# Expert outputs collected in two ways: the first 40 experts through zeroed rows that are summed during the last twelve pairs, the other 24 through three sums in DRAM

## The chip, the core and the metric

The kernel runs on one core of a Trainium2 chip. TensorE (PE) multiplies and transposes, VectorE (DVE) and ScalarE (ACT) work on tiles, GpSimd (POOL) issues the indirect DMAs, and SyncE (SP) issues most of the others. SBUF is the on-chip memory with 128 partitions, PSUM receives what PE computes, DRAM lies outside. The metric is the time of one execution in microseconds, lower is better; each version is timed in several executions and the median counts.

## What is computed

One transformer block on x of shape (2, 512, 256): 1024 tokens of 256 channels. A mixing layer comes first, then a mixture of 64 small experts, of which each token uses 6, beside a shared expert that all tokens use. Cut to what matters here:

```python
router_logits = x @ gate_w.T
probs = softmax(router_logits)                      # 1024 x 64
topk_w, topk_idx = top_k(probs, 6)
topk_w = topk_w / sum(topk_w)
combine = sum(one_hot(topk_idx, 64) * topk_w[..., None], axis=1)
h = silu(einsum('th,eih->tei', x, experts_w1))      # 64 experts, 176 wide
y = einsum('tei,ehi->teh', h, experts_w2)
routed_out = einsum('teh,te->th', y, combine)
ffn = routed_out + shared_out
out = x + layernorm(ffn)
```

Only the six chosen experts of a token are computed. So every token has six rows of 256 numbers, made by six experts at different times, and these have to be added before the last layernorm.

## The kernel before

**Mixing and routing (0 to 136 us of the span).** Eight tiles of 128 tokens pass through the mixing layer, get their router logits and their top six. Each tile then sends its token rows to the experts: `xs_d` in DRAM has 1024 row places for each expert, and six indirect DMAs (scatters, line 576) per tile write each token's row to the next free place of each of its experts, 48 scatters in all. A row (`ROW` = 384 floats, 1536 bytes) holds the 256 normalized channels, 64 combine weights and 64 integers. The integer of expert e says which row of `y_d` the output for this token and expert belongs to: row 6 x token + k. A scan over the chosen experts (`tok[:, t, DEST:]`) makes these numbers. Before that, the first 128 places of each expert are filled with `blank`, a row with zero weights and row numbers that are out of bounds, so that empty places write nothing.

On SP's queue stand, in this order: the inputs, four fills of `xs_d` with `blank` (line 173), the shared expert's weights, the weights of the first 11 pairs of experts, a copy of the token rows to `tok_d` in two halves (lines 706 and 719) with the weights of pairs 11 and 12 between them, and then the loop's loads.

**Expert pairs (136 to 266 us).** 32 pairs of experts, two at a time, in a software pipeline that is written out by hand. In step n of the loop at the end of `block_kernel`:

- SP issues the load of pair n + 4 from `xs_d` (`load`, tile `xg`, five buffers);
- `turn_h` transposes the hidden values of pair n - 2 on PE and copies them to SBUF on DVE (lines 921 to 925);
- `turn` transposes the token rows of pair n on PE (line 887); DVE copies the weight and row-number columns (`cols`, line 891) and the transposed rows (`xT`, line 893);
- `up` multiplies pair n - 1 by its first weights (line 906), ACT applies SiLU (lines 911 and 912);
- `down` multiplies pair n - 2 by its second weights (lines 933 and 937), ACT scales by the combine weights (line 940) into `y`, which has six buffers, and `collect` issues one indirect DMA per expert that writes its up to 128 rows to `y_d` (line 864). These are the puts, two for each pair;
- SP issues further weights, until all are loaded.

An expert with more than 128 tokens has its surplus computed by `further`, one extra block of 128 rows spread over steps 3 to 8 of the loop. After the loop stands a hardware loop (`tc.For_i`, line 1007) for still more surplus, which turns zero times with this data. All engines and all DMAs meet at it.

**Tail (272 us to the end).** For each of the eight token tiles, 768 KB of `y_d` (six rows for each token) are loaded into `yk`, half by a DMA of SP and half by one of ACT (line 1021); these wait for every put. `total_up` adds the upper three rows to the lower three on DVE (line 1032), and PE adds `y_sh` (the shared expert, line 1029) and the three sums (line 1034) by multiplying with the identity and accumulating in PSUM. `measure` takes mean and variance, `put_out` normalizes, adds x and writes the tile out (line 1057); for the last two tiles this is done on DVE, for the others on ACT and POOL.

Of the kernel before, what the change touches and what calls it, by code (L numbers as in the profile page):

```python
# [10 lines left out]
F32 = mybir.dt.float32  # L11
BF16 = mybir.dt.bfloat16
I32 = mybir.dt.int32
# [5 lines left out]
P = 128  # L19
# [16 lines left out]
FLOAT = 1  # L36
G = 2
NG = E // G
DEST = C + E
ROW = DEST + E  # L40
WROW = 2 * I + C
HALF = P // 2
SEL = 131072.0
# [9 lines left out]
def block_kernel(ctx: ExitStack, tc, x, w_act, w_rec, w_val, gate, wa, wb, wb_one, sh_gu, sh_dn, out):  # L53
# [110 lines left out]

    blank = const.tile([P, ROW], F32, name="blank")
    nc.gpsimd.memset(blank[:, :DEST], 0.0)
    nc.gpsimd.iota(blank[:, DEST:].bitcast(I32), pattern=[[0, E]], base=int(FAR), channel_multiplier=0)


    xs_d = dram.tile([E * CAP, ROW], F32, name="xs_d")  # L170
# [10 lines left out]

    
    first_i = const.tile([P, NTT], I32, name="first_i")
    for i in range(NTT):
        nc.gpsimd.iota(
# [157 lines left out]
    def spent(n):  # L345
        return 0.16 + n / 960
# [93 lines left out]

    hsh = carve(len(SH_CHUNKS), NT)
    tok = carve(NTT, ROW)
    sel = data.tile([P, NTT, E], BF16, name="sel")
    lg = data.tile([P, NTT, E + 10], F32, name="lg")
    nc.gpsimd.memset(lg[:, :, E : E + 2], NEG)
    none_sel = const.tile([P, E], BF16, name="none_sel")
# [26 lines left out]
    def token_tile(t, pv):  # L473
# [79 lines left out]
        for j in range(t):  # L553
# [5 lines left out]
        yield spent(E / 2)  # L559

        nc.vector.tensor_tensor_scan(
            tok[:, t, DEST:].bitcast(I32), sel[:, t, :], none_sel, first_f[:, t : t + 1], ALU.add, ALU.add
        )
        yield spent(2 * E)

        nc.vector.reciprocal(tsum, tsum)
        nc.scalar.activation(comb, comb, AF.Copy, scale=tsum)
# [188 lines left out]
    def further(now, f):  # L756
# [64 lines left out]
        nc.vector.tensor_mul(two, xg[:, C:DEST], one)  # L821
        wt = stat.tile([P, 1], F32, tag="wt", name="wt")
        nc.vector.tensor_reduce(wt, two, AX.X, ALU.add)
        nc.vector.tensor_mul(two, xg[:, DEST:].bitcast(I32), one)
        to = stat.tile([P, 1], F32, tag="to", name="to")
        nc.vector.tensor_reduce(to, two, AX.X, ALU.add)
        to_i = stat.tile([P, 1], I32, tag="to_i", name="to_i")
        nc.vector.tensor_copy(to_i, to)
        yield
        px = ps.tile([P, KC, P], F32, tag="ps", name="px")  # L830
        for k in range(KC):
# [19 lines left out]
        nc.tensor.matmul(py, hT[:IB, 1, :], wb_f, start=False, stop=True)  # L851
        y = hpool.tile([P, C], F32, tag="y_f", name="y_f", bufs=1)
        nc.scalar.activation(y, py, AF.Copy, scale=wt)
        collect(y, to_i)
        yield

    def after_scatters(ins):
# [5 lines left out]
    def collect(y, rows):  # L863
# [10 lines left out]
        tc.add_to_no_dep_group("puts", ins)  # L874
        puts.append(ins)

    def load(g):
        xg = hpool.tile([P, G, ROW], F32, tag="xg", name="xg", bufs=5)
        after_scatters(nc.sync.dma_start(xg, xs_v[:P, g * G : (g + 1) * G, :]).ins)
        return xg  # L880

    def turn(xg, g):

        px = ps.tile([P, G, KC, P], F32, tag="pr", name="px", bufs=1)
        for q in range(G):
            for k in range(KC):
                nc.tensor.transpose(px[:, q, k, :], xg[:, q, ts(k, P)], ident)  # L887
        cols = hpool.tile([P, 2, G], F32, tag="cols", name="cols", bufs=12)
        flat = xg.rearrange("p q r -> p (q r)")
        for u, o in enumerate((C + g * G, DEST + g * G)):  # L890
            nc.vector.tensor_copy(cols[:, u, :].bitcast(I32), flat[:, o : o + ROW + 2 : ROW + 1].bitcast(I32))
        xT = hpool.tile([P, G, KC, P], F32, tag="xT", name="xT")
        nc.vector.tensor_copy(xT, px)  # L893
        return xT, cols
# [30 lines left out]
        nc.vector.tensor_copy(hT[: HALF + IB, G, :], pt[: HALF + IB, G, :])  # L925
        return hT

    def down(hT, w2as, w2b, wts, rows):

        pys = []  # L930
        for q in range(G):
            py = ps.tile([P, C], F32, tag="ps", name="py")
            nc.tensor.matmul(py, hT[:, q, :], w2as[q], start=True, stop=False)  # L933
            pys.append(py)
        for q in range(G):
            lo = q * HALF
            nc.tensor.matmul(pys[q], hT[lo : lo + IB, G, :], w2b[lo : lo + IB, :], start=False, stop=True)  # L937
        y = hpool.tile([P, G, C], F32, tag="y", name="y", bufs=6)
        for q in range(G):
            nc.scalar.activation(y[:, q, :], pys[q], AF.Copy, scale=wts[q])  # L940
            collect(y[:, q, :], rows[q])


    floats = []
# [16 lines left out]
    warm = ps.tile([P, C], F32, tag="ps", name="warm")  # L961
    for i in range(5):
        nc.tensor.matmul(warm, ident, x_sb[:, 0, :], start=(i == 0), stop=(i == 4))

    AHEAD = 4
    xgs, xTs, hs, hTs, cols = {}, {}, {}, {}, {}
# [3 lines left out]
    for n in range(NG + 2):  # L970
        if n + AHEAD < NG:
            xgs[n + AHEAD] = load(n + AHEAD)
        if FIRST + 2 + n < FIRST + SECOND:
            load_weights(FIRST + 2 + n)
        if 0 <= n - 2 < NG:
            hTs[n - 2] = turn_h(hs.pop(n - 2))
        if n < NG:
            xTs[n], cols[n] = turn(xgs.pop(n), n)
        float_step(n)
        if 0 <= n - 1 < NG:  # L980
            wa_sb, wb_sb = weights[n - 1]
            hs[n - 1] = up(xTs.pop(n - 1), [wa_sb[:, q, : 2 * I] for q in range(G)])
        if 0 <= n - 2 < NG:
            m = n - 2
            wa_sb, wb_sb = weights[m]
            col = cols.pop(m)
            down(
                hTs.pop(m),
                [wa_sb[:, q, 2 * I :] for q in range(G)],
                wb_sb,  # L990
                [col[:, 0, q : q + 1] for q in range(G)],
                [col[:, 1, q : q + 1] for q in range(G)],
            )
# [13 lines left out]
    with tc.For_i(0, left, 1):  # L1007
# [4 lines left out]

    hstack.close()
    tpool = ctx.enter_context(tc.tile_pool(name="tpool", bufs=3))
    y_v = y_d.rearrange("(i p k) c -> p i k c", k=TOPK, p=P)
    half = TOPK // 2
    yks, pos, mvs, rstds = {}, {}, {}, {}
    for i in range(NTT):
        yks[i] = tpool.tile([P, TOPK, C], F32, tag="yk", name="yk", bufs=NTT)
        for eng, o in ((nc.sync, 0), (nc.scalar, half)):  # L1020
            ins = eng.dma_start(yks[i][:, o : o + half, :], y_v[:, i, o : o + half]).ins
            for w in puts:
                tc.add_manual_dep(ins, w.name, SYNC, reason="reads what every block wrote")

    def total_up(i):

        yk = yks.pop(i)
        po = pos[i] = ps.tile([P, C], F32, tag="ps", name="po")
        nc.tensor.matmul(po, ident, y_sh[:, i, :], start=True, stop=False)
        pieces = [(0, half)] if i < NTT - 2 else [(k, k + 1) for k in range(half)]  # L1030
        for o, u in pieces:
            nc.vector.tensor_add(yk[:, o:u, :], yk[:, o:u, :], yk[:, half + o : half + u, :])  # L1032
        for k in range(half):
            nc.tensor.matmul(po, ident, yk[:, k, :], start=False, stop=(k == half - 1))  # L1034

    def measure(i):
        mv = mvs[i] = stat.tile([P, 2], F32, tag="mv_o", name="mv_o")
# [69 lines left out]
```

## Time and profile before

| | us |
|---|---|
| median of 4 runs | 301.35 |
| lowest and highest run | 298.26 and 301.86 |
| the profiled execution | 301.84 |
| its span, first to last instruction | 300.1 |
| mean granted TensorE clock | 0.886 |

The profile's times are us from the start of the span. Busy shares of the span are PE 80%, DVE 50%, ACT 40% and POOL 42%, but they mix three stages with different limits: the mixing stage, where chains between engines alternate and the DMA queues are full for the first 75 us, the pair loop, and the tail. The stages are read one by one with the view that gives the busy time of each engine in chosen stretches, and with the timeline. In the view of waits, the longest wait of the pair loop is this one:

```profile
DVE hT L924 <- PE pht L922: 67.6, 30, 3.5
```

It says that DVE waited 67.6 us in total, in 30 of the 32 steps, for PE's transposes of the hidden values.

### The profile page before, as it was taken

Reading aid. Unit: us, or ns where it says so; the run is one execution under the profiler, and the core shown is the slowest. Engines: PE = TensorE matmul, PEld = TensorE weight load, DVE = VectorE, ACT = ScalarE, POOL = GpSimd, SP = SyncE. Lnnn points to the kernel's source line nnn. Section 1 sums busy time; section 2 is a strip of 40 time slices with the busy share of each in tenths; the row PEclk is TensorE's granted clock in tenths of the full one; section 3 lists DMA queues with packets and bytes.
Section 4 is the critical chain, followed back from the end, with each engine's and each line's share of the span. In section 5 each row is a group of like instructions: output and inputs, shape, how many; then the busy total and the mean of one; then the engine's idle time right before and its main releaser. Section 6 shows DMA issues by size and latency. Waiting matters only on the chain. (4 is left out here: it accounts for less than half of the span.)

```text
span 300.1 us, 4388 instructions
## 1 busy us (share of the span) xinstructions
PE 239.3 (80%) x1258; PEld 190.0 (63%) x1258; DVE 149.6 (50%) x628; ACT 120.0 (40%) x341; POOL 125.3 (42%) x159
## 2 busy tenths in 40 slices
PE   1989824954877929995898999999999999921992
PEld 0778613843665717874676778888888877710881
DVE  3569899756768503760345323344433333201594
ACT  3494665256127336502134444433333333320241
POOL 6000006723741761773064465555555555550041
PEclk9999975887597775995999999999999999995697
DMA  7999999999662440637999999999855531115982
GB/s 227 379 401 400 389 331 347 394 387 327 263 221 99 157 155 35 233 131 261 352 344 352 358 362 364 363 357 346 264 159 154 155 116 54 54 54 203 407 307 79
DMA packets 44025, 77.58 MB, mean 259 GB/s; under 512 B 4885, under 2 KB 29578, under 8 KB 44000
## 3 DMA queue, kind: packets, MB, share of 16 engines
q1 hardware_dynamic: 36480, 58.04, 56.6%
q0 software_dynamic: 6368, 16.11, 14.6%
q10 hardware_dynamic: 1152, 3.15, 2.9%
q8 instruction: 10, 0.16, 0.2%
q14 instruction: 15, 0.12, 0.1%
HBM read 46.53 MB, written 33.16 MB: 266 GB/s over the span
## 5 line engine op out<-in xcount | busy, mean ns | idle before, releaser
L864 POOL DMA_INDIRECT y_d<-y,cols x64 | 63.1, 987 | 66.2 <-ACT y L940 54.1
L576 POOL DMA_INDIRECT xs_d<-arena,slot_i x48 | 48.0, 999 | 81.3 <-ACT lg L526 40.9
L924 DVE COPY hT<-pht 128x256 f32<-128x256 f32 x32 | 13.6, 424 | 69.2 <-PE pht L922 67.6
L940 ACT ACTIVATE y<-py,cols 128x256 f32<-128x256 f32 x64 | 26.8, 470 | 29.2 <-PE py L937 27.4
L911 ACT ACTIVATE h<-ph 128x256 f32<-128x256 f32 x32 | 12.3, 383 | 47.7 <-PE ph L906 40.1
L906 PE MATMUL ph<-w_sb,xT 128*128 128x176 f32 x176 | 30.0, 313 | 0.0
L599 PE MATMUL pgu<-x2T,sh_gu_sb 128*128 128x256 f32 (+1 forms) x96 | 27.9, 453 | 0.0
L906 PEld LDWEIGHTS ph<-w_sb,xT 128*128 128x128 f32 x176 | 26.4, 190 | 0.3 <-issue 0.3
L893 DVE COPY xT<-px 128x512 f32<-128x512 f32 x32 | 21.9, 685 | 4.3 <-PE px L887 4.3
L599 PEld LDWEIGHTS pgu<-x2T,sh_gu_sb 128*128 128x128 f32 (+1 forms) x96 | 20.4, 217 | 4.9
L395 DVE TENSOR_TENSOR m<-z 128x32 f32<-128x32 f32 (+7 forms) x92 | 22.0, 281 | 2.4 <-remote 1.8
L933 PE MATMUL py<-w_sb,hT 128*128 128x256 f32 x88 | 22.7, 380 | 0.0
L458 PE MATMUL pv<-w_val_sb,z 128*128 128x256 f32 x32 | 12.7, 565 | 11.7 <-DVE z L398 7.8
L887 PE MATMUL px<-ident,xg 128*128 128x128 f32 x128 | 19.3, 273 | 0.8 <-DVE xT L893 0.8
L264 PE MATMUL pz<-xnT,arena 128*128 128x256 f32 x64 | 17.4, 434 | 1.7 <-ACT xnT L253 1.0
L458 PEld LDWEIGHTS pv<-w_val_sb,z 128*128 128x128 f32 x32 | 8.6, 281 | 14.1 <-issue 9.8
L1034 PE MATMUL po<-yk,ident 128*128 128x256 f32 x48 | 14.1, 436 | 3.7 <-DVE yk L1032 3.7
L264 PEld LDWEIGHTS pz<-xnT,arena 128*128 128x128 f32 x64 | 13.8, 220 | 4.9 <-ACT xnT L253 1.4
L933 PEld LDWEIGHTS py<-w_sb,hT 128*128 128x128 f32 x88 | 15.8, 190 | 1.2
L887 PEld LDWEIGHTS px<-ident,xg 128*128 128x128 f32 x128 | 15.0, 141 | 1.2 <-DVE xT L893 1.0
L921 PE MATMUL pht<-ident,h 128*128 128x128 f32 x64 | 14.0, 301 | 2.0 <-ACT h L911 2.0
L283 PE MATMUL pr<-arena,xnT 128*128 128x256 f32 x64 | 15.5, 398 | 0.0
(203 smaller groups left out, 428.5 us busy)
## 6 DMA issues: line engine op xcount, KB each, us to landing
w_sb<-in_wa SPq DMA_DIRECT2D x22, 608.0 KB
xs_d<-blank SPq DMA_DIRECT2D x4, 3072.0 KB
xg<-xs_d SPq DMA_DIRECT2D x32, 384.0 KB
arena<-in_wa SPq DMA_DIRECT2D x10, 608.0 KB
yk<-y_d ACTq DMA_DIRECT2D x8, 384.0 KB
yk<-y_d SPq DMA_DIRECT2D x8, 384.0 KB
w_sb<-in_wb SPq DMA_DIRECT2D x22, 112.0 KB
tok_d<-arena SPq DMA_DIRECT2D x2, 768.0 KB
```

The source lines that it names most:

```text
L264: nc.tensor.matmul(pz[:, ri, :], w_act_sb[:, kk, ts(ri, P)], xnT[:, kk % KC, b, o : o + H], start=(kk == 0), stop=(kk == 3),)
L283: nc.tensor.matmul(pr[:, j, :], xnT[:, kk % KC, b, o : o + P], w_rec_sb[:, kk, :], start=(kk == 0), stop=(kk == 3),)
L395: nc.vector.tensor_mul(h, dst, low[:, u : u + 1].to_broadcast(shape))
L458: nc.tensor.matmul(pv, zs[c][:, ri, 1 + j * P : 1 + (j + 1) * P], w_val_sb[:, ri, :], start=(ri == 0), stop=(ri == 1),)
L576: ins = nc.gpsimd.indirect_dma_start(out=xs_d[:, :], out_offset=bass.IndirectOffsetOnAxis(ap=slot_i[:, t, k : k + 1].bitcast(U32), axis=0) ...
L599: nc.tensor.matmul(pgu[:n, u, :], sh_gu_sb[:, k, off : off + n], x2T[:, k, ts(c, H)], start=(k == 0), stop=(k == KC - 1),)
L864: ins = nc.gpsimd.indirect_dma_start(out=y_d[:, :], out_offset=bass.IndirectOffsetOnAxis(ap=rows.bitcast(U32), axis=0), in_=y, in_offset=None,
L887: nc.tensor.transpose(px[:, q, k, :], xg[:, q, ts(k, P)], ident)
L893: nc.vector.tensor_copy(xT, px)
L906: nc.tensor.matmul(ph[:, q, :], xT[:, q, k, :], w1[:, ts(k, I)], start=(k == 0), stop=(k == KC - 1))
L933: nc.tensor.matmul(py, hT[:, q, :], w2as[q], start=True, stop=False)
L940: nc.scalar.activation(y[:, q, :], pys[q], AF.Copy, scale=wts[q])
```

## The change

1. Two kinds of output. Pairs 0 to 19 (experts 0 to 39, `LO`) write to `y_d` as before. Pairs 20 to 31 and the extra block use `add_up`: an indirect DMA that adds its rows to one of three sums of 1024 x 256 floats in DRAM (`s0_d` to `s2_d`), taken in turn. An add must wait until the add before it in the same sum has landed.
2. Since a token's six experts are now split between both kinds, unused rows of `y_d` must be zero: a fill of 6 MB zeroes `y_d`, three of 1 MB zero the sums. They stand on SP's queue behind the weights of the first 11 pairs.
3. The row becomes 361 floats (1444 bytes): row numbers for 40 experts, and one column with the token's number, which the adds use. The scans get shorter, and `further` no longer works out a row number.
4. `y_d` is read during the last twelve pairs: `load_low` loads a token tile's 768 KB (steps 20 to 27 counted by the finished pair m) after all puts of the first 20 pairs, into SBUF that held weights of earlier pairs, and `sum_low` adds it into `y_sh` with four DVE instructions per tile, three or four of them in each step from m = 22 on.
5. The tail loads 3 x 128 KB for each tile, 24 DMAs in all, of which ACT issues four and SP twenty. DVE adds two of the three, PE multiplies three times where it did four times.
6. PE gets idle multiplications (`keep_warm`): 14 after the last pair, 6 before the tail, besides the 5 that there were. ACT loads the table for the square root ahead of its first use.

```diff
+LO, NACC = 40, 3
-ROW = DEST + E
+ROW = DEST + LO + 1
 ...
+    nc.sync.dma_start(
+        y_d.rearrange("(i p) c -> p i c", p=P), blank[:, :C].unsqueeze(1).to_broadcast([P, NTT * TOPK, C])
+    )
+    sums = [dram.tile([NT, C], F32, name=f"s{a}_d") for a in range(NACC)]
+    sums_v = [s_d.rearrange("(i p) c -> p i c", p=P) for s_d in sums]
+    for s_v in sums_v:
+        nc.sync.dma_start(s_v, blank[:, :C].unsqueeze(1).to_broadcast([P, NTT, C]))
 ...
-        nc.vector.tensor_mul(two, xg[:, DEST:].bitcast(I32), one)
-        to = stat.tile([P, 1], F32, tag="to", name="to")
-        nc.vector.tensor_reduce(to, two, AX.X, ALU.add)
-        to_i = stat.tile([P, 1], I32, tag="to_i", name="to_i")
-        nc.vector.tensor_copy(to_i, to)
 ...
-        collect(y, to_i)
+        add_up(y, src)
 ...
+    def add_up(y, tokens):
+        nc.gpsimd.indirect_dma_start(
+            out=sums[next(sum_turns)][:, :],
+            out_offset=bass.IndirectOffsetOnAxis(ap=tokens.bitcast(U32), axis=0),
+            in_=y,
+            in_offset=None,
+            bounds_check=NT - 1,
+            oob_is_err=False,
+            compute_op=ALU.add,
+        )
+    LAST_LO = LO // G - 1
+    LBUF = 5
+    def load_low(i):
+        o = 2 * PAIR + (i % LBUF) * TOPK * C
+        yk = lows[i] = arena[:, o : o + TOPK * C].rearrange("p (k c) -> p k c", k=TOPK)
+        ins = nc.sync.dma_start(yk, y_v[:, i]).ins
+        for w in puts:
+            tc.add_manual_dep(ins, w.name, SYNC, reason="reads what the first blocks wrote")
+    def sum_low(i):
+        yk = lows.pop(i)
+        nc.vector.tensor_add(yk[:, :half, :], yk[:, :half, :], yk[:, half:, :])
+        yield
+        nc.vector.tensor_add(yk[:, 0, :], yk[:, 0, :], yk[:, 1, :])
+        yield
+        nc.vector.tensor_add(y_sh[:, i, :], y_sh[:, i, :], yk[:, 2, :])
+        yield
+        nc.vector.tensor_add(y_sh[:, i, :], y_sh[:, i, :], yk[:, 0, :])
+        yield
 ...
+                collect if m <= LAST_LO else add_up,
 ...
+            if 0 <= m - LAST_LO - 1 < NTT:
+                load_low(m - LAST_LO - 1)
+            for _ in range(0 if m < LAST_LO + 3 else 4 if m < LAST_LO + 5 else 3):
+                next(low_sums, None)
 ...
+    keep_warm(14)
     nc.scalar.copy(count, total)
 ...
-        yks[i] = tpool.tile([P, TOPK, C], F32, tag="yk", name="yk", bufs=NTT)
-        for eng, o in ((nc.sync, 0), (nc.scalar, half)):
-            ins = eng.dma_start(yks[i][:, o : o + half, :], y_v[:, i, o : o + half]).ins
+        yks[i] = tpool.tile([P, NACC, C], F32, tag="yk", name="yk", bufs=NTT)
+        for a in range(NACC):
+            (nc.scalar if issued % 2 and issued < 8 else nc.sync).dma_start(yks[i][:, a, :], sums_v[a][:, i, :])
+            issued += 1
+    nc.scalar.preload_act_table_set("sqrt_and_others")
+    keep_warm(6)
 ...
         nc.tensor.matmul(po, ident, y_sh[:, i, :], start=True, stop=False)
-        pieces = [(0, half)] if i < NTT - 2 else [(k, k + 1) for k in range(half)]
-        for o, u in pieces:
-            nc.vector.tensor_add(yk[:, o:u, :], yk[:, o:u, :], yk[:, half + o : half + u, :])
-        for k in range(half):
-            nc.tensor.matmul(po, ident, yk[:, k, :], start=False, stop=(k == half - 1))
+        nc.vector.tensor_add(yk[:, 0, :], yk[:, 0, :], yk[:, 1, :])
+        nc.tensor.matmul(po, ident, yk[:, 2, :], start=False, stop=False)
+        nc.tensor.matmul(po, ident, yk[:, 0, :], start=False, stop=True)
```

More of the change, by code (lines that the diff above doesn't have):

```diff
@@ L166, in block_kernel @@
     nc.gpsimd.memset(blank[:, :DEST], 0.0)
-    nc.gpsimd.iota(blank[:, DEST:].bitcast(I32), pattern=[[0, E]], base=int(FAR), channel_multiplier=0)
+    nc.gpsimd.iota(blank[:, DEST:].bitcast(I32), pattern=[[0, ROW - DEST]], base=int(FAR), channel_multiplier=0)
     xs_d = dram.tile([E * CAP, ROW], F32, name="xs_d")
@@ L442, in block_kernel @@
     tok = carve(NTT, ROW)
+    nc.gpsimd.iota(tok[:, :, ROW - 1 :].bitcast(I32), pattern=[[P, NTT], [0, 1]], base=0, channel_multiplier=1)
     sel = data.tile([P, NTT, E], BF16, name="sel")
@@ L445, in block_kernel @@
     nc.gpsimd.memset(lg[:, :, E : E + 2], NEG)
-    none_sel = const.tile([P, E], BF16, name="none_sel")
+    none_sel = const.tile([P, LO], BF16, name="none_sel")
     nc.gpsimd.memset(none_sel, 0.0)
@@ L561, in token_tile @@
         nc.vector.tensor_tensor_scan(
-            tok[:, t, DEST:].bitcast(I32), sel[:, t, :], none_sel, first_f[:, t : t + 1], ALU.add, ALU.add
+            tok[:, t, DEST : ROW - 1].bitcast(I32), sel[:, t, :LO], none_sel, first_f[:, t : t + 1], ALU.add, ALU.add
         )
-        yield spent(2 * E)
+        yield spent(2 * LO)
         nc.vector.reciprocal(tsum, tsum)
@@ L875, in collect @@
         puts.append(ins)
+    sum_turns = cycle(range(NACC))
+    def add_up(y, tokens):
[9 more added lines that the diff above has]
+    LAST_LO = LO // G - 1
+    y_v = y_d.rearrange("(i p k) c -> p i k c", k=TOPK, p=P)
+    half = TOPK // 2
+    LBUF = 5
+    lows = {}
+    def load_low(i):
+        o = 2 * PAIR + (i % LBUF) * TOPK * C
+        assert o + TOPK * C <= SECOND * PAIR
+        yk = lows[i] = arena[:, o : o + TOPK * C].rearrange("p (k c) -> p k c", k=TOPK)
[12 more added lines that the diff above has]
+        yield
+    low_sums = (step for i in range(NTT) for step in sum_low(i))
     def load(g):
@@ L889, in turn @@
         flat = xg.rearrange("p q r -> p (q r)")
-        for u, o in enumerate((C + g * G, DEST + g * G)):
-            nc.vector.tensor_copy(cols[:, u, :].bitcast(I32), flat[:, o : o + ROW + 2 : ROW + 1].bitcast(I32))
+        o = C + g * G
+        nc.vector.tensor_copy(cols[:, 0, :], flat[:, o : o + ROW + 2 : ROW + 1])
+        o = DEST + g * G
+        to = flat[:, o : o + ROW + 2 : ROW + 1] if g <= LAST_LO else xg[:, :, ROW - 1]
+        nc.vector.tensor_copy(cols[:, 1, :].bitcast(I32), to.bitcast(I32))
         xT = hpool.tile([P, G, KC, P], F32, tag="xT", name="xT")
@@ L926, in turn_h, with down @@
         return hT
-    def down(hT, w2as, w2b, wts, rows):
+    def down(hT, w2as, w2b, wts, rows, put):
         pys = []
@@ L940, in down @@
             nc.scalar.activation(y[:, q, :], pys[q], AF.Copy, scale=wts[q])
-            collect(y[:, q, :], rows[q])
+            put(y[:, q, :], rows[q])
     floats = []
@@ L958, in float_step, with keep_warm @@
             next(floats[f])
-    warm = ps.tile([P, C], F32, tag="ps", name="warm")
-    for i in range(5):
-        nc.tensor.matmul(warm, ident, x_sb[:, 0, :], start=(i == 0), stop=(i == 4))
+    def keep_warm(n):
+        warm = ps.tile([P, C], F32, tag="ps", name="warm")
+        for i in range(n):
+            nc.tensor.matmul(warm, ident, x_sb[:, 0, :], start=(i == 0), stop=(i == n - 1))
+    keep_warm(5)
     AHEAD = 4
@@ L1014, in block_kernel @@
     tpool = ctx.enter_context(tc.tile_pool(name="tpool", bufs=3))
-    y_v = y_d.rearrange("(i p k) c -> p i k c", k=TOPK, p=P)
-    half = TOPK // 2
     yks, pos, mvs, rstds = {}, {}, {}, {}
+    issued = 0
     for i in range(NTT):
-        yks[i] = tpool.tile([P, TOPK, C], F32, tag="yk", name="yk", bufs=NTT)
-        for eng, o in ((nc.sync, 0), (nc.scalar, half)):
-            ins = eng.dma_start(yks[i][:, o : o + half, :], y_v[:, i, o : o + half]).ins
-            for w in puts:
-                tc.add_manual_dep(ins, w.name, SYNC, reason="reads what every block wrote")
+        yks[i] = tpool.tile([P, NACC, C], F32, tag="yk", name="yk", bufs=NTT)
[4 more added lines that the diff above has]
+    keep_warm(6)
     def total_up(i):
```

## The prediction

> **What bounds the kernel now.** The chain of waits on the page covers only the last 1.1 us, so I read the stages one by one. First the view of busy time by stretches, cut at the stage borders (columns: from:to and length in us, busy time and count of PE, PEld, DVE, ACT, POOL, granted clock, DMA share, GB/s):
>
> ```profile
> 160.00:180.00 20.00, 20.00 (x125) 15.65 (x124) 8.46 (x33) 9.03 (x27) 10.87 (x11) 1.00 1.05 359
> 217.00:232.00 15.00, 15.00 (x98) 12.14 (x97) 6.01 (x24) 5.45 (x16) 8.44 (x9) 1.00 0.53 162
> 232.00:247.00 15.00, 15.00 (x97) 12.12 (x96) 5.72 (x21) 5.45 (x16) 8.14 (x10) 1.00 0.43 130
> 266.00:272.50 6.50, 0.00 (x0) 0.00 (x0) 0.00 (x0) 0.14 (x2) 1.98 (x2) 0.76 0.15 51
> 272.50:286.00 13.50, 9.41 (x27) 7.09 (x28) 5.65 (x11) 2.44 (x4) 0.55 (x1) 0.61 0.95 357
> ...
> 75.00:118.00 43.00, 31.89 (x140) 24.59 (x141) 23.57 (x121) 17.02 (x63) 20.80 (x22) 0.74 0.43 157
> ...
> 229.00:254.00 25.00, 25.00 (x162) 20.02 (x161) 9.52 (x35) 9.54 (x28) 13.65 (x14) 1.00 0.38 117
> ```
>
> In the pair loop PE never rests, with the DMA engines full (160 to 180) as with them half empty (217 to 247): the loop is bound by PE, and from 217 on there is DMA time to spare. Then 6.5 us of nothing, and a tail that begins with a DMA stage on a slow clock. The seam is in GpSimd's timeline:
>
> ```profile
> 256.44 0.98 POOL L864 DMA_INDIRECT y_d<-y,cols  x1 [1.33 <-ACT y L940]
> 257.72 0.99 POOL L864 DMA_INDIRECT y_d<-y,cols  x1 [0.30 <-DVE xT L893]
> 260.04 0.98 POOL L864 DMA_INDIRECT y_d<-y,cols  x1 [1.33 <-ACT y L940]
> ...
> 267.45 0.99 POOL L864 DMA_INDIRECT y_d<-y,cols  x1 [1.97 <-ACTq L1007]
> 268.75 0.99 POOL L864 DMA_INDIRECT y_d<-y,cols  x1 [0.30 <-POOLq L1007]
> ```
>
> Two puts in a pair, 1.3 us apart, a pair every 3.61 us (the same spot comes at 252.83 and 256.44); the last one starts at 268.75, and the tail's loads start at 272.52, in the timeline of the tail:
>
> ```profile
> 272.52 10.24 ACTq L1021 DMA_DIRECT2D yk<-y_d  x8
> ...
> 276.79 0.96 DVE L1032 TENSOR_TENSOR yk<-yk 128x768 f32<-128x768 f32 x1 [13.22 <-DMA yk<-y_d]
> ...
> 285.22 0.59 PE L1029 MATMUL po<-y_sh,ident 128*128 128x256 f32 x2
> 285.71 1.56 PE L1034 MATMUL po<-yk,ident 128*128 128x256 f32 x6
> ...
> 292.72 1.46 PE L1034 MATMUL po<-yk,ident 128*128 128x256 f32 x6
> ...
> 296.75 0.43 DVE L1055 TENSOR_TENSOR o_sb<-o_sb,x_sb 128x256 f32<-128x256 f32 x1
> ```
>
> From first load to last DVE end: 297.18 - 272.52 = 24.66 us. Data take 4.27 us to arrive; once they flow, a tile costs 1.77 us (tile 3's PE group starts at 285.22, tile 7's at 292.29; four in 7.07), eight PE passes of 0.22, with DVE nearly as full.
>
> **The tail gets shorter.** PE makes three multiplications for a tile instead of four: 1.77 x 3/4 = 1.33 us. Before them stand six idle ones, two passes each: 12 x 0.22 = 2.65 us, from 0.4 us after the first load (272.93 before). The last tile is thus through PE 0.4 + 2.65 + 8 x 1.33 = 13.7 us after the first load. From PE's end to the last DVE end before took 297.18 - 294.21 = 2.97, and this stays: 16.65 us in all. DVE needs 0.36 + 0.43 + 0.18 + 0.13 + 0.16 = 1.26 us a tile, under PE's 1.33. Data: 24 x 131 KB at the 357 GB/s of the tail's row is 8.8 us plus some 2.1 us until the first arrive (4.27 less 0.79 MB at that rate), so about 11, then 0.4 for the add, 0.5 for the last multiplication and 2.97: 15. PE's sum is later and counts: 24.66 - 16.65 = **8.0 us gained**. Bounds: 9.6, if only the data set the end; 5.5, if the idle multiplications run on the slow clock, as the five before the pair loop did (ten passes in 4.35 us, so 12 cost 5.2, 2.5 more). The 14 other idle ones lie in the gap: 28 x 0.22 = 6.2 us from 265.2 end at 271.4, before all engines meet.
>
> **The adds, unknown.** No row shows an add. A plain indirect write lands 2.71 us after its start (last scatter at 133.63, the loads that wait for it at 136.34) to at most 3.55 us (last put at 268.75 until 272.3, the meeting of the engines included). An add also reads its destination: at best hidden, at worst in series with the 2.1 us a tail load needs besides its bytes. So L, start to landing, is between 2.71 and 5.6; I take 4.6, nearer to the serial case, since a sum cannot be written before it is read. The last add lands 4.6 - 3.55 = **1.0 us later** (-0.8 to +2.1).
>
> Each add waits on GpSimd for the add three before. Behind it stand only other adds; ACT waits for them through `y`'s six buffers, six pairs or 22 us later, so a lag costs at the end alone. The second of the 24 adds would start at 231.2 and the last at 268.75: seven turns of its sum in 37.6 us, 5.37 each. With L below 5.37 nothing slips, above it 7 x (L - 5.37). In that stretch DMAs fill: 117 GB/s of the row at 229 plus 0.79 MB per 3.61 us (218) plus the adds' reads (2 x 98 KB per 3.61 us, 54) is 389, above the 359 of the full stretch. A gather there took 5.81 us (issued at 154.28, used at 160.09). At that L the slip is 3.1 us; the last four pairs have little traffic and catch up. I take **1.0 us** (0 to 3.1).
>
> The Trainium skill, "DMA: Bandwidth & Descriptors", section "Latency and other measured facts", gives 2 us for an HBM access at high load: an estimate of L by it is 3.55 + 2 = 5.55, a slip of 1.3 us; no run here shows it.
>
> **Summing within the loop, 0.** Eight tiles of 0.96 + 3 x 0.36 = 2.04 us are 16.3 us of DVE. Cover: in each pair DVE idles 2.25 us behind PE's transposes; three steps cost at most 1.68, four 2.04. Loads are in time: the last put of pair 19 starts at 225.26 and lands near 228.8, 0.79 MB follow by about 233.5, and the first sum stands behind `xT` of pair 24, near 235.9. SP waits there with the load of pair 27 behind it, needed four steps later. Without cover a late load stalls DVE and PE; I allow 0 to 1 us.
>
> **Fills, 0.** 9.44 MB at 370 to 390 GB/s are 24 to 25.5 us of DMA. The stretch 75 to 118 has a share of 0.43, so 24.5 us are free, and nothing in it waits for a load. SP is held in the fills until about 95; behind it stand `tok_d` (issued at 71.71, read by the gather at 154) and two pairs' weights that are used much later. What spills beyond 118 meets the last twelve scatters: first rows are there at 140.26, PE wants them at 143.3, so 3 us are covered. 0 to 3 us lost.
>
> **Shorter rows, 0.** 6% fewer bytes in fills, scatters and loads, all under cover (the loop is bound by PE). The first scatter starts at 46.3 and the fill is through near 40, so a slower one is covered too. Against it speaks the Trainium skill, the same page, section "How a descriptor splits into AXI transactions": a piece not starting on 256 bytes costs an extra transaction, so 1444 bytes take up to seven where 1536 took six. By it the 12.6 MB of fill cost up to 5 us more instead of 2 less; the sum stays, since both are hidden.
>
> **Extra block.** Three DVE steps of 0.22 + 0.22 + 0.15 = 0.59 us go, between the late gather (160.09) and the next `hT` for which PE waits: **0.5 us gained** (0 to 0.6).
>
> **Sum.** 8.0 + 0.5 - 1.0 - 1.0 = 6.5 us. The profiled execution took 301.84 (span 300.1), so 295.3; the median shown is 0.5 lower: **294.8**.
>
> **Rivals.**
> - *The adds take GpSimd's place as the bound (slower).* Cost against a plain put: (L - 3.55) + 7 x (L - 5.37), gain elsewhere 8.5; they balance at L = 6.2. At L = 7 it is 3.5 + 11.4 - 8.5 = 6.4 us, so 307.7. For: full DMAs where most of the adds run, and 5.81 for a mere read there. Against: idle rows give at most 5.6, and the last pairs are quiet. 0.21.
> - *The tail is bound by SP's issues (no change).* SP issues 20 loads; five of its eight before took 4.26 us, 0.85 each, and 20 would take 17 us, the last data 2.1 later and 3.9 of work: 23 us, a gain of 1.7, eaten by the adds: 301. Against: single issues take 0.33, the rest were waits for landings. With the cold PE and a full slip (-5.5 + 2.1 + 3.1 - 0.5) it is 300.6, the same outcome. 0.13.
> - *The fills delay the last scatters.* 3 us of the gain go: 297.8. 0.08.
>
> The forecast itself 0.58.
>
> **How the numbers follow.** 1% (3 us) is about what a measurement of this kernel, whose runs lie between 298.3 and 301.9, can tell from no change. Faster by more: forecast and fills, 0.66. Within: 0.13. Slower: 0.21. All bounds in favour (9.6 + 0.8 + 0.6) give 290.4; upwards the range takes in the no-change cases and the mild end of the adds: **290 to 303**.
>
> **What would show it.** Right: GpSimd's adds start at ACT's pace up to the last one; the tail's loads within 2 us of 272.5; about 1.3 us between tiles in the tail and some 17 us for it; pairs still 3.61 us apart from 20 to 31. Wrong: adds that wait for DMAs and drift behind `y`; DVE waiting for the arena loads and PE for `hT`; SP's issues 0.8 us apart in the tail; `xg` landing after 143.

## The result and the profile after

| | before | after |
|---|---|---|
| median, us | 301.18 (32 runs) | 311.99 (22 runs) |
| lowest and highest run, us | 298.26 and 306.22 | 307.47 and 322.29 |
| the profiled execution, us | 301.84 | 309.44 |
| its span, us | 300.1 | 307.7 |
| mean granted TensorE clock | 0.886 | 0.891 |

The change makes the kernel slower: the ratio of the times is 1.0296, with a 95% interval of 1.0266 to 1.0326. (Disturbed executions, some per cent longer, are left out of the ratio, so it isn't the quotient of the two medians; the profiles of e1, e4 and e10 are of such executions, and are read here by single stretches.) The prediction of 294.8 us and its range up to 303 are missed. The outcome is that of the rival on the other side (slower); the 307.7 us that it gave lie below the 311.99.

The profiled executions are 7.6 us apart. Three cuts show where that is: the end of ACT's last `y` of the pair loop, the first load of the tail, and the last DVE instruction.

| | before | after | difference |
|---|---|---|---|
| start to the end of ACT's last `y` | 266.06 | 264.76 | -1.3 |
| from there to the tail's first load | 6.46 | 20.09 | +13.6 |
| from there to the last DVE end | 24.66 | 20.06 | -4.6 |

So the pair loop is not slower, the tail has gained something, and the seam between them has become three times as long. First the busy time by stretches of the kernel after (columns as in the prediction: from:to and length, busy time and count of PE, PEld, DVE, ACT, POOL, granted clock, DMA share, GB/s):

```profile
7.50:37.50 30.00, 26.45 (x116) 22.07 (x116) 22.66 (x86) 19.33 (x40) 0.00 (x0) 1.00 1.05 334
75.00:118.00 43.00, 32.20 (x145) 25.29 (x146) 23.10 (x121) 17.66 (x67) 20.36 (x21) 0.74 1.05 366
...
217.00:232.00 15.00, 15.00 (x96) 11.79 (x94) 6.43 (x22) 5.87 (x18) 9.41 (x8) 1.00 0.60 182
232.00:247.00 15.00, 15.00 (x97) 11.87 (x96) 13.09 (x36) 5.46 (x16) 8.05 (x5) 1.00 1.07 367
...
272.50:280.00 7.50, 0.00 (x0) 0.00 (x0) 0.00 (x0) 0.00 (x0) 6.24 (x4) 0.64 0.51 53
280.00:290.00 10.00, 4.51 (x11) 3.58 (x12) 0.42 (x1) 1.28 (x1) 1.56 (x1) 0.50 0.56 137
...
242.00:246.00 4.00, 4.00 (x27) 3.23 (x26) 3.48 (x10) 1.63 (x5) 2.45 (x2) 1.00 1.09 363
246.00:250.00 4.00, 4.00 (x26) 2.99 (x24) 3.47 (x10) 1.62 (x6) 2.23 (x2) 1.00 1.06 371
250.00:254.00 4.00, 4.00 (x28) 3.19 (x27) 2.84 (x9) 1.37 (x4) 1.56 (x1) 1.00 0.69 214
254.00:258.00 4.00, 4.00 (x28) 3.01 (x25) 3.26 (x9) 1.38 (x5) 2.28 (x2) 1.00 0.51 79
```

From 232 to 247 DVE's busy time goes from 5.72 to 13.09 us of 15, and PE is still busy for all 15.00: the sums in the loop are hidden. The DMA share there goes from 0.43 to 1.07, with the loads of `y_d`; they are issued between 226.46 and 242.5, and the four last rows show that the engines stay full until about 250. From 272.5 to 280 only GpSimd has anything to do: four adds, and nothing that the other engines could do before them. Here is GpSimd's timeline (start and length, the operation, in brackets the idle time before it and what ended it):

```profile
226.27 1.58 POOL L886 DMA_INDIRECT s_d<-y,cols  x1 [1.33 <-ACT y L990]
...
234.69 1.56 POOL L886 DMA_INDIRECT s_d<-y,cols  x1 [3.07 <-issue]
...
243.25 1.56 POOL L886 DMA_INDIRECT s_d<-y,cols  x1 [3.02 <-DMA s_d<-y,cols]
245.11 1.56 POOL L886 DMA_INDIRECT s_d<-y,cols  x1 [0.30 <-issue]
...
251.97 1.56 POOL L886 DMA_INDIRECT s_d<-y,cols  x1 [2.79 <-ACT y L990]
254.37 1.56 POOL L886 DMA_INDIRECT s_d<-y,cols  x1 [0.84 <-DVE y_sh L917]
...
261.17 1.56 POOL L886 DMA_INDIRECT s_d<-y,cols  x1 [0.30 <-DMA s_d<-y,cols]
263.04 1.78 POOL L886 DMA_INDIRECT s_d<-y,cols  x1 [0.31 <-issue]
...
278.43 1.56 POOL L886 DMA_INDIRECT s_d<-y,cols  x1 [0.56 <-DMA s_d<-y,cols]
280.30 1.56 POOL L886 DMA_INDIRECT s_d<-y,cols  x1 [0.30 <-DMA s_d<-y,cols]
```

Each add uses the sum of the third add before it and must wait until that one has landed. The 1st, 4th, 7th and 10th add start at 226.27, 234.69, 243.25 and 251.97: 8.4, 8.6 and 8.7 us apart. The 8th starts at 245.11 and the 11th at 254.37, 9.3 us later. (Where a bracket names ACT or DVE, it is only the last event that the trace saw: the `y` for the add at 251.97 comes four pairs after that for the first one, at about 240.7, 11 us before.) From about 259 on the adds follow each other without a pause, 1.86 us apart (1.56 for the instruction and 0.30 before it), three of them in 5.6. The last one starts at 280.30, 11.55 us later than before's last put, and its data have landed when the loads start at 284.85, 4.55 us later. The groups of the page give the two instructions beside each other, the put (L870) and the add (L886):

```profile
L870 POOL DMA_INDIRECT y_d<-y,cols x40 | 39.6, 990 | 45.4 <-ACT y L990 38.9
L886 POOL DMA_INDIRECT s_d<-y,cols x24 | 38.1, 1589 | 18.8 <-ACT y L990 5.7
```

The add takes GpSimd 1.6 times as long as the put. Before's busy times from 247 to 266, where the puts are almost alone on the DMA engines, are there to compare with after's from 272.5 to 280, where the adds are alone:

```profile
247.00:266.00 19.00, 17.67 (x107) 13.09 (x105) 5.32 (x19) 7.60 (x23) 10.72 (x11) 1.00 0.16 57
```

Then the timeline of the tail:

```profile
284.85 10.96 SPq L1080 DMA_DIRECT2D yk<-s_d  x20
285.49 5.49 PE L1014 MATMUL warm<-x_sb,ident 128*128 128x256 f32 x12 [15.36 <-issue]
287.29 0.42 DVE L1091 TENSOR_TENSOR yk<-yk 128x256 f32<-128x256 f32 x1 [23.90 <-DMA yk<-s_d]
...
290.77 1.01 PE L1090 MATMUL po<-y_sh,ident 128*128 128x256 f32 x2
292.48 0.59 PE L1090 MATMUL po<-y_sh,ident 128*128 128x256 f32 x2
293.78 0.59 PE L1090 MATMUL po<-y_sh,ident 128*128 128x256 f32 x2
295.07 0.59 PE L1090 MATMUL po<-y_sh,ident 128*128 128x256 f32 x2
...
304.49 0.42 DVE L1114 TENSOR_TENSOR o_sb<-o_sb,x_sb 128x256 f32<-128x256 f32 x1
```

The tiles follow each other after 1.30 us, the predicted 1.33. But the twelve idle passes ahead of them, behind 15.36 us without work, take 5.49 us at a granted clock of 0.50, and DVE had the first two sums of the first tile at 287.29, 3.5 us before PE begins on it.

### The profile page after: what moved, and what is told of

It reads as the page before. It is cut to its first block, busy times and chain, and to the rows that moved or that the text cites. A ratio compares the mean times of both kernels' runs of the same rounds, so it can differ in the third digit from the quotient of the medians.

```text
span 307.7 us, 4469 instructions
## 1 busy us (share of the span) xinstructions
PE 240.6 (78%) x1282; PEld 193.1 (63%) x1282; DVE 161.2 (52%) x653; ACT 120.4 (39%) x341; POOL 140.0 (45%) x160
## 5 line engine op out<-in xcount | busy, mean ns | idle before, releaser
L870 POOL DMA_INDIRECT y_d<-y,cols x40 | 39.6, 990 | 45.4 <-ACT y L990 38.9
L886 POOL DMA_INDIRECT s_d<-y,cols x24 | 38.1, 1589 | 18.8 <-ACT y L990 5.7
L974 DVE COPY hT<-pht 128x256 f32<-128x256 f32 x32 | 13.6, 424 | 52.7 <-PE pht L972 50.7
L1014 PE MATMUL warm<-x_sb,ident 128*128 128x256 f32 x50 | 15.8, 484 | 15.4 <-issue 15.4
L610 PE MATMUL pgu<-x2T,sh_gu_sb 128*128 128x256 f32 (+1 forms) x96 | 26.3, 434 | 0.0
L1014 PEld LDWEIGHTS warm<-x_sb,ident 128*128 128x128 f32 x50 | 12.0, 247 | 18.4 <-issue 16.1
L610 PEld LDWEIGHTS pgu<-x2T,sh_gu_sb 128*128 128x128 f32 (+1 forms) x96 | 19.7, 210 | 4.5
L274 PE MATMUL pz<-xnT,arena 128*128 128x256 f32 x64 | 16.4, 417 | 1.7 <-ACT xnT L263 1.0
L1091 DVE TENSOR_TENSOR yk<-yk 128x256 f32<-128x256 f32 x8 | 3.3, 416 | 26.3 <-DMA yk<-s_d 26.3
```

The costliest lines, as they stand in the source:

```text
L274: nc.tensor.matmul(pz[:, ri, :], w_act_sb[:, kk, ts(ri, P)], xnT[:, kk % KC, b, o : o + H], start=(kk == 0), stop=(kk == 3),)
L610: nc.tensor.matmul(pgu[:n, u, :], sh_gu_sb[:, k, off : off + n], x2T[:, k, ts(c, H)], start=(k == 0), stop=(k == KC - 1),)
L870: ins = nc.gpsimd.indirect_dma_start(out=y_d[:, :], out_offset=bass.IndirectOffsetOnAxis(ap=rows.bitcast(U32), axis=0), in_=y, in_offset=None,
L886: nc.gpsimd.indirect_dma_start(out=sums[next(sum_turns)][:, :], out_offset=bass.IndirectOffsetOnAxis(ap=tokens.bitcast(U32), axis=0), in_= ...
```

## The experiments

The theory after the result: **the adds wait for the adds before them in the same sum, and these land late because the loads of `y_d` fill the DMA engines at the same time; beside that the add's own instruction is longer than a put's.** Against it stood the sums on DVE, a queue of GpSimd's own, the read of the destination in itself, the fills and the shorter rows. Each run is read by two lengths of its trace: the pair stage, from the start of ACT's first `y` to the end of its last, and the seam, from there to the tail's first load.

| run | pair stage, us | seam, us | median, us | ratio to before |
|---|---|---|---|---|
| before | 115.2 | 6.5 | 301.18 | |
| after | 115.3 | 20.1 | 311.99 | 1.0296 [1.0266, 1.0326] |
| e1, no loads and sums in the loop | 117.1 | 10.6 | 303.37 | 1.0009 [0.9955, 1.0063] |
| e2, six sums | 121.1 | 8.8 | 306.36 | 1.0163 [1.0078, 1.0248] |
| e3, plain writes for adds | 119.8 | 7.6 | 305.55 | 1.0156 [1.0059, 1.0254] |
| e4, more idle passes | 115.6 | 19.8 | 313.42 | 1.0306 [1.0192, 1.042] |
| e9, after once more | 115.1 | 20.1 | 314.85 | 1.0383 [1.028, 1.0486] |
| e8, late fills | 118.6 | 18.4 | 313.88 | 1.0416 [1.034, 1.0492] |

Ratios are to runs of before on the same chip in the same session: 302.66 us with e1 to e4, 301.04 with e8 to e10 and v2. In the session of e5 to e7 and v1 before took 286.72; of that below.

**e1: the first 40 experts' outputs are neither read nor summed.** Puts, fills and adds stay.

```diff
-            if 0 <= m - LAST_LO - 1 < NTT:
-                load_low(m - LAST_LO - 1)
-            for _ in range(0 if m < LAST_LO + 3 else 4 if m < LAST_LO + 5 else 3):
-                next(low_sums, None)
```

> Leaves out the loads of y_d and their sums, so the outputs of the first 40 experts are missing. Theory A (an add lands in 8 to 10 us instead of 5 because the bulk loads of y_d keep the DMA engines full, and the adds wait for each other): without the loads the adds follow each other at 1.86 us, the last starts near 269 to 271 instead of 280.3, the tail's loads start near 274 to 275 instead of 284.9, the time falls by 9 to 11 us to about 301. Rival B (three chained adds are slow in themselves, whatever else runs): the last add still starts after 278 and the time falls by at most 2 us. Rival C (the 16 us of sums on VectorE hold the pairs up): the pairs of 20 to 31 come closer together than 3.6 us.

The seam falls from 20.1 to 10.6 us. GpSimd's timeline of e1, and below it a stretch of its busy times:

```profile
234.64 1.58 POOL L886 DMA_INDIRECT s_d<-y,cols  x1 [1.33 <-DMA xg<-xs_d]
236.53 1.58 POOL L886 DMA_INDIRECT s_d<-y,cols  x1 [0.31 <-ACT h L961]
238.42 1.57 POOL L886 DMA_INDIRECT s_d<-y,cols  x1 [0.30 <-DMA s_d<-y,cols]
240.29 1.56 POOL L886 DMA_INDIRECT s_d<-y,cols  x1 [0.30 <-DMA s_d<-y,cols]
...
279.33 1.56 POOL L886 DMA_INDIRECT s_d<-y,cols  x1 [0.30 <-DMA s_d<-y,cols]
```

```profile
242.00:246.00 4.00, 4.00 (x27) 3.29 (x27) 1.82 (x10) 1.36 (x4) 3.12 (x2) 1.00 0.77 141
```

The fourth add now starts 5.65 us after the first, which is three instructions without a pause, at a DMA share of 0.77 instead of 1.09. So 9.5 us of the lost 13.6 come from what e1 leaves out, and 4.1 from the adds themselves: from first to last start they take 23 x 1.86 = 42.8 us where before's puts took 41.2 (227.58 to 268.75), some 1.9 us go into short pauses (279.33 - 234.64 = 44.7), and the last lands 4.40 us after its start instead of 3.77.

e1 leaves out loads and DVE sums together. The four last rows of the windows of after part them: from 254 to 258 DVE is busy with sums for 3.26 us of 4, as it was from 242 to 250, but the loads are over (79 GB/s), and there the waits end. The adds of 257.28 and 259.18 find theirs done after 5.8 and 6.0 us, where the ones of 245.11 and 247.63 needed 9.3 and 9.7. The loads are the cause, by this reading; no run has the loads without the sums throughout, but a stretch of e7 has, and it says the same (below).

**e2: six sums for the adds, of which the tail reads three.** Half of the adds are left out of the output, and there are three more fills of 1 MB.

```diff
-LO, NACC = 40, 3
+LO, NACC, NSUM = 40, 3, 6
-    sums = [dram.tile([NT, C], F32, name=f"s{a}_d") for a in range(NACC)]
+    sums = [dram.tile([NT, C], F32, name=f"s{a}_d") for a in range(NSUM)]
-    sum_turns = cycle(range(NACC))
+    sum_turns = cycle(range(NSUM))
```

> Adds go in turn into six sums instead of three; the tail still loads three, so what went into the other three is missing from the output. An add waits for the add six before. Theory A and B alike (the wait for landing is what delays, not GpSimd's own 1.56 us): 6 x 1.86 = 11.2 us is more than the 8 to 10 us of a landing, so adds follow each other at 1.86 us or at ScalarE's pace, the last starts at 269 to 271 and the time falls by 9 to 11 us. Rival D (GpSimd's longer instruction alone sets the end): nothing changes, the last add starts near 280.

The adds no longer wait for each other while the loads run. In GpSimd's timeline of e2 the first six go without a pause, with the loads as in after:

```profile
239.03 1.56 POOL L886 DMA_INDIRECT s_d<-y,cols  x1 [0.30 <-DMA arena<-y_d]
240.90 1.56 POOL L886 DMA_INDIRECT s_d<-y,cols  x1 [0.30 <-ACT y L990]
242.76 1.57 POOL L886 DMA_INDIRECT s_d<-y,cols  x1 [0.30 <-ACT h L962]
246.29 1.76 POOL L886 DMA_INDIRECT s_d<-y,cols  x1 [1.96 <-ACT y L990]
```

So it is the wait for the same sum that costs, and not a queue on GpSimd. The seam is 8.8 us, but the time is only 1.6% above before and not level with it: the pair stage is 5.9 us longer. Two waits of PE in it are new, 1.82 us at 243.75 for DVE's `hT` and 1.17 us at 185.08 for token rows; the first is what the prediction had named for a load that comes late to DVE. The rest of the 5.9 us is in gaps below 1 us that were not followed up.

**e3: the same instruction without the addition**, so that rows of a sum overwrite each other; loads, sums and waits stay.

```diff
             oob_is_err=False,
-            compute_op=ALU.add,
```

> The adds become plain indirect writes into the same sums with the same waits; a later row replaces an earlier one, so the output lacks the sums. Theory A with the cost in reading and adding: the instruction falls from 1.56 to 0.98 us, a landing under the loads takes 5 us or less, the last write starts near 268 to 270, the time falls by 10 to 12 us. Rival E (the waits and the full DMA engines cost the same for a plain write): landings stay at 7 us or more while the loads run, the last write starts after 274, the time falls by less than 6 us.

```profile
228.34 0.98 POOL L886 DMA_INDIRECT s_d<-y,cols  x1 [1.33 <-ACT y L989]
...
234.08 1.14 POOL L886 DMA_INDIRECT s_d<-y,cols  x1 [1.15 <-ACT h L961]
...
243.85 2.07 POOL L886 DMA_INDIRECT s_d<-y,cols  x1 [1.87 <-ACT y L989]
...
252.14 0.98 POOL L886 DMA_INDIRECT s_d<-y,cols  x1 [3.48 <-ACT h L961]
```

GpSimd's timeline of e3 shows the 0.98 us of a put again, and waits beside the loads all the same: the fourth starts 5.7 us after the first, the eleventh after a pause of 3.48 us and 8.3 us after the eighth. So plain writes land late there too, in 5.7 to 8.3 us where the adds needed 8.4 to 9.7. But they are short enough to catch up afterwards, and the seam is 7.6 us. The theory was half right here: full DMA engines delay any indirect write; that the delay is still there at the end needs the longer add. The pair stage is 4.5 us longer; in it PE stands for 2.52 us at 263.35, until ACT's `h` at 265.44, which itself comes after 4.30 us of idle time with no releaser that the trace could name; what caused that stays open.

**e4: 30 more idle multiplications** before the meeting of the engines.

```diff
-    keep_warm(14)
+    keep_warm(44)
```

> 44 idle multiplications after the last pair instead of 14, so that TensorE stays busy until about 283.6, near the start of the tail. Theory F (the tail's gain was 4.6 us instead of 8.0 since the clock had fallen while TensorE stood still from 270.1 to 285.5): the first six idle multiplications of the tail take 2.7 us instead of 5.5, the tail 17 us instead of 20, the time falls by 2.5 to 3.5 us. Rival G (the tail waits for its data): the tail stays within 1 us of 20 us.

The tail takes 18.8 us where it took 20.06 in the profile of after. But e9, the unaltered program, took 18.7 us for it, with 4.49 us for the same twelve idle passes behind 15.38 us without work. In e4 PE stands still for only 2.05 us ahead of them, and they take as long:

```profile
292.77 4.54 PE L1014 MATMUL warm<-x_sb,ident 128*128 128x256 f32 x12 [2.05 <-issue]
```

The expected 2.7 us did not come, and the granted clock from 294 to 296 is 0.50. So the long pause is not what makes these passes slow; what does stays open.

**e5: before, with the four fills of after** (9.4 MB into memory that nothing reads), at the same place in SP's queue. e6, e7 and v1 ran in the same session, in which the granted clock from 75 to 118 was 0.91 to 0.94 instead of 0.74, and the last scatter comes near 118 instead of 134.

```diff
+    z_d = dram.tile([NT * TOPK, C], F32, name="z_d")
+    nc.sync.dma_start(
+        z_d.rearrange("(i p) c -> p i c", p=P), blank[:, :C].unsqueeze(1).to_broadcast([P, NTT * TOPK, C])
+    )
+    for a in range(3):
+        s_d = dram.tile([NT, C], F32, name=f"s{a}_d")
+        nc.sync.dma_start(
+            s_d.rearrange("(i p) c -> p i c", p=P), blank[:, :C].unsqueeze(1).to_broadcast([P, NTT, C])
+        )
```

> The kernel before with the four zero fills (9.4 MB) at the place they have in the changed kernel, into memory that nothing reads. Theory H (the fills cost 2 to 5 us in the mixing stage, because the DMA engines stay full to 118 us and the engines stand still there with nothing to show but missing instructions): the time rises by 2 to 5 us, the first puts start 2 to 5 us after 151.6. Rival I (the fills are covered, and the later start of the loop in the last runs is chance or comes from the shorter rows): the time stays within 1 us of before.

297.24 us against 286.72, ratio 1.0387 [1.0331, 1.0443]: the fills cost 10.5 us here. The busy times of e5, and then of v1, which has none of the fills:

```profile
75.00:118.00 43.00, 39.34 (x204) 32.06 (x204) 30.88 (x157) 24.17 (x78) 28.07 (x30) 0.91 1.05 367
118.00:136.00 18.00, 4.70 (x28) 3.46 (x26) 0.45 (x3) 0.59 (x1) 4.14 (x7) 0.74 1.01 346
```

```profile
75.00:118.00 43.00, 39.15 (x206) 31.96 (x205) 30.91 (x157) 24.16 (x78) 28.21 (x30) 0.92 0.57 215
118.00:136.00 18.00, 12.99 (x77) 10.84 (x76) 4.94 (x20) 3.10 (x9) 4.97 (x8) 0.91 0.88 305
```

Up to 118 the engines do the same work in both. Then, in e5, the DMA engines are still full (1.01) while PE works 4.70 us of 18: the last scatter starts at 118.76, but the loads of the first pairs' rows only at 127.82, against 117.95 and 120.66 in v1.

**e10: the same program as e5** in a session in which its clock from 75 to 118 is 0.74, as in the prediction's profile, beside e9, which is after unaltered.

> The kernel before with the fills once more. Theory H2 (the fills end near 118 to 125 whatever the clock, and cost what they stand beyond the last scatter): with the mixing stage ending near 118 the time rises by 9 to 12 us, with its end near 134 by 0 to 4 us. Rival (the fills cost a fixed amount by slowing every engine): 10 us in either case.

> The changed kernel unaltered, beside its parts on one chip. If the mixing stage ends near 118 (granted clock 0.9 in 75 to 118), fills and adds both count: 1.06 to 1.075 of before. If it ends near 134 (clock 0.74), the fills are mostly covered: 1.025 to 1.04.

305.04 us against 301.04, ratio 1.0058 [0.9968, 1.0148]: no difference that can be told. The last scatter starts at 134.29 and the loads of the rows at 137.00, 2.7 us later. The fills are the same; what covers them is longer by 16 us. e9 repeats after's seam and pair stage.

**e8: the fills of two sums moved** from SP's early queue to step 14 of the pair loop.

```diff
-    for s_v in sums_v:
+    for s_v in sums_v[:1]:
...
+            if m == 14:
+                for s_v in sums_v[1:]:
+                    nc.sync.dma_start(s_v, blank[:, :C].unsqueeze(1).to_broadcast([P, NTT, C]))
```

> The fills of the second and third sum are issued in the loop, after pair 14, when SyncE has no weights left to load; the fills of y_d and of the first sum stay. Theory H2: the first puts come 5 to 6 us earlier than in the changed kernel where the mixing stage ends near 118, and the time falls by as much; 0 to 3 us where it ends near 134. Rival: no change, since the engines wait for something else.

1.0416 beside e9's 1.0383, with intervals that overlap widely: nothing gained, as e10 says for this clock.

**e6: rows of 1536 bytes as before**, the 40 row numbers and the token's number in their old width.

```diff
-ROW = DEST + LO + 1
+ROW = DEST + E
```

> The changed kernel with rows of 384 floats again (1536 bytes, the middle columns unused). If rows of 1444 bytes slow the fill of the expert rows (320 to 337 GB/s after against 360 to 393 before): that stretch returns to 360 to 390 GB/s and the first scatter starts near 46 again. Theory J: the mixing stage is shorter for it and the time falls by 1 to 3 us against the changed kernel. Rival K (covered): the time stays within 1 us of the changed kernel's ratio of 1.03.

The fill of `xs_d`, from 7.5 to 37.5, in e6 and then in before:

```profile
7.50:37.50 30.00, 26.32 (x116) 21.93 (x116) 23.06 (x88) 19.55 (x40) 0.00 (x0) 1.00 1.06 388
7.50:37.50 30.00, 27.37 (x116) 22.68 (x116) 22.50 (x86) 18.69 (x38) 0.00 (x0) 1.00 1.05 392
```

388 GB/s, where after had 334 at the same share of the DMA engines and before 392. The first scatter starts at 46.75 instead of 52.23 (46.28 before). The time is 305.19 us or 1.0635 [1.0563, 1.0706]; after itself was not run beside it. But e7 has after's rows and differs from after only from pair 20 on: ACT's first `y` starts at 145.55 in e7 and at 145.70 in e6. The gain in the fill is covered by then, as the prediction had it.

**e7: three buffers for the loads of `y_d` instead of five**, so that they come spread out.

```diff
-    LBUF = 5
+    LBUF = 3
```

> Three buffers instead of five for the loads of y_d, so that they spread over the pairs instead of running ahead. Theory A (full DMA engines make each add land later): fewer bytes beside the adds of the pairs 21 to 25, landings of 6 to 7 us instead of 8 to 10, from the first add to the tail's loads 53 to 56 us instead of 58.5, the time falls by 2 to 5 us. Rival L (the waits only move to the later adds): 58 us as now, no gain.

307.6 us, 1.0684 [1.0598, 1.0769]; one of its four executions took 1289.59 us, and why stays open. Nothing is gained, but the edit does more than spread the loads. With three buffers tile 5 is loaded into the buffer of tile 2 (step 25) before the last sum of tile 2 has its turn, and likewise tiles 6 and 7 into those of tiles 3 and 4. These sums must then wait for the new load, and they add its rows, so part of the output is wrong. The busy times of e7, and its timeline of DVE and GpSimd:

```profile
232.00:247.00 15.00, 11.24 (x69) 8.57 (x69) 7.18 (x21) 4.09 (x12) 9.31 (x6) 1.00 1.01 330
241.50:248.30 6.80, 1.74 (x13) 1.47 (x11) 0.00 (x0) 1.02 (x4) 4.68 (x3) 0.98 0.81 235
```

```profile
241.56 1.56 POOL L886 DMA_INDIRECT s_d<-y,cols  x1 [1.95 <-issue]
...
248.38 0.43 DVE L919 TENSOR_TENSOR y_sh<-y_sh,arena 128x256 f32<-128x256 f32 x1 [8.13 <-DMA arena<-y_d]
249.29 1.81 POOL L886 DMA_INDIRECT s_d<-y,cols  x1 [1.55 <-DMA s_d<-y,cols]
```

The last sum of tile 2 waits 8.13 us for a load of `y_d`, `hT` stands behind it on DVE, and PE waits 7.28 us for `hT` at 250.52 and 3.00 us at 263.60; the pair stage is 131.8 us long. So e7 does not test the spreading. The seam is short (8.1 us) because the adds catch up meanwhile. But the stall parts what e1 left together: from 241.5 to 248.3 DVE does nothing while loads go on (235 GB/s on the mean), and the add of 241.56 still keeps the third one after it waiting until 249.29, 7.7 us, with the last 1.55 put down to its DMA.

**Two versions.** v1 is before with what the change does for the tail and the loop does not need: 14 and 8 idle multiplications, the table for the square root loaded ahead, four of ACT's eight loads on SP.

```diff
+    keep_warm(14)
     nc.scalar.copy(count, total)
...
+    keep_warm(8)
...
-        for eng, o in ((nc.sync, 0), (nc.scalar, half)):
+        for eng, o in ((nc.sync, 0), (nc.scalar if i < 4 else nc.sync, half)):
...
+    nc.scalar.preload_act_table_set("sqrt_and_others")
```

> The kernel before with only the idle multiplications (14 after the last pair, 8 before the tail), the early table load of ScalarE and four of its eight tail loads moved to SyncE; the outputs are collected as before. If TensorE's slow clock and the late table load hold up the first tiles of the tail: 24.7 us of tail become 22 to 23.5, the time falls by 1 to 2.5 us. Rival (the tail waits for its 6.3 MB): no difference that can be measured.

286.54 us against 286.72, ratio 0.9961 [0.9919, 1.0003]. Its tail takes 23.4 us, e5's unchanged one in the same session 25.7, but the time can't be told from no change. v2 is after with e8's fills, e6's rows and 40 idle multiplications.

> The changed kernel with the late fills, rows of 384 floats and 40 idle multiplications after the last pair. By the theories so far: 5 to 8 us faster than the changed kernel where the mixing stage ends early (fills 5, warm tail 2, rows 0 to 1), 2 to 5 us where it ends late; slower than before in both, since the adds' 12 us at the end of the loop are not touched.

309.99 us, 1.0331 [1.0264, 1.0398]: still slower, with a seam of 21.5 us. No version beats before beyond doubt.

## Why the prediction was wrong, step by step

**The adds: wrong, and this is the step that failed.** "The adds, unknown" took 4.6 us from start to landing, at most 5.6, and charged 2.0 us for landing and slip together. The seam became 13.6 us longer. Three things were off:

- 4.6 us is right for an add with no other traffic beside it (4.55 for the last one, the meeting of the engines included). But the ones that others paused for run while the loads fill the DMA engines, and need 8.4 to 9.7 us. The upper end of 5.6 was built from the last put (a DMA share of 0.15 from 266 to 272.5) and the tail's first loads, which start when nothing else is under way; the price came from another stage than the one it was for.
- The check on the traffic added GB/s, 389 against 359, and found the DMAs 8% overbooked. In engine time it is far more. Adds alone, 272.5 to 280 of after, hold a share of 0.51 for 53 GB/s; before's puts, 247 to 266, held 0.16 for 57 GB/s, a third. Adds without a pause take 0.5, and per pair a load of 768 KB and one of 361 KB come to 320 GB/s, which by after's row from 75 to 118 (1.05 for 366, no adds in it) is a share of 0.92. Together that is an estimate of 1.4; it is a rough one, since shares measured apart need not add up, and the rows at 242 and 246, with both in them, show 1.09 and 1.06.
- The instruction was taken as a put's 0.98 us. It takes 1.56, and two of them with their pauses, 3.72 us, are more than a pair's 3.61. So "the last four pairs have little traffic and catch up" could not be: there is no idle time on GpSimd to catch up in. e1 shows this part nearly alone: 4.1 us, of which 0.6 are the landing of the last add.

The rival's mechanism, adds that wait for late landings, was the right one for 9.5 of the 13.6 us, with 0.21; the longer instruction was not in it. Its formula gives the measured 13.6 us at a mean landing of 6.8 us (8 L = 13.6 + 3.55 + 7 x 5.37), between the 9.7 beside the loads and the 5.6 behind them. Its balance at 6.2 us lay too high, since the adds cost 4.1 us without any late landing and the tail gained only 4.6.

The Trainium skill, "DMA: Bandwidth & Descriptors", section "Latency and other measured facts", gives 2 us for an HBM access at high load, from which the prediction had its estimate of 5.55 us. The 8.4 to 9.7 us measured beside the loads are beyond it.

**The tail: right in its mechanism, wrong in size.** 4.6 us gained instead of 8.0, below the lower bound of 5.5; in e9 it was 6.0 (18.7 us). Of the 3.4 us missing, 2.6 are the idle passes, which ran on the slow clock (0.50); that was in the prediction's lower bound, but not in its value. They stand behind 15.36 us without work that GpSimd's late adds leave, but e4 shows them as slow behind 2.05 us. The rest is 0.2 to 0.3 us each at the start, over the eight tiles and at the end. The tiles, 1.30 us each, came as worked out. The rival of SP's issues is out: 20 in 10.96 us, 0.55 each.

**Summing within the loop: right.** The pair stage is 115.3 us where it was 115.2. DVE's adds of 256 took 0.42 us instead of 0.36, without effect. That the cover is thin is shown by e2, where DVE's first sum waits 3.06 us for its load and PE then 1.82 us for `hT`.

**Fills: within the bound for the clock it was made from**, as far as e10 can tell (its interval allows up to 4.5 us), and wrong elsewhere: with a granted clock of 0.91 in the same stage they cost 10.5 us. The prediction looked for readers of the filled memory and for free DMA time, and not for what would be left if the stage ended earlier. SP is held in the fills until 106.7 in after, not until about 95.

**Shorter rows: right.** They are slower and hidden. By the bytes and GB/s of the rows from 7.5 to 37.5, a row of 1444 bytes takes 1444/334 where one of 1536 took 1536/392, a ratio of 1.10; e6 undoes it. The skill's rule in "How a descriptor splits into AXI transactions", same page, fits: an estimate by it is seven transactions for five of eight rows and six for the others, against six, a ratio of 1.10, below the 1.17 of "up to seven".

**Extra block: not to be told.** ACT's first `y` starts 1.4 us earlier than before in the profile of after, and 0.7 us later in e9.

## What to carry to other kernels

Price a chained DMA with the landing that it has under the traffic of its own stage, and add up the traffic in DMA engine time, not in bytes. Before an operation is counted as able to catch up, hold its own issue time against the period of the loop that feeds it. A transfer that is covered by a stage is covered only up to that stage's end, which here lay near 118 us in the session with a granted clock of 0.91 to 0.94 and near 134 with 0.74.

## What was not expected of the hardware

- An indirect DMA that adds takes GpSimd 1.56 us where the plain one takes 0.98, and three times its share of the DMA engines for the same bytes (0.51 at 53 GB/s against 0.16 at 57).
- Beside DVE's sums the plain writes of e3 stretched on GpSimd from 0.98 to as much as 2.07 us. The loads alone do not do it: the three adds of e7 between 241.56 and 247.74, beside loads but no sum, took 1.56 us each, and after's add of 263.04, beside a sum when the loads were over, 1.78. Not every write beside a sum is stretched.
- The granted clock from 75 to 118 is 0.74 to 0.83 in some sessions and 0.91 to 0.94 in another, and before then takes 301 or 287 us. What makes the difference was not tried.
- Idle multiplications did not keep PE at full clock across the meeting of the engines: in v2, after 17.53 us of them and a pause of 5.40 us, the twelve passes ahead of the tail still took 4.84 us, and in e4, after 19.26 us and a pause of 2.05 us, 4.54, against 2.65 at full clock. In v1 sixteen passes behind a pause of 2.04 us took 3.50 us, at a clock of 1.00. What makes the difference was not tried.
